# A first attention whose spare steps follow a fixed plan, with the shared expert of two blocks among them

## The chip, the cores and the metric

One core of a Trainium2 chip. The metric is the device time of one execution in microseconds (us). Engine names are those of the profile: PE is TensorE (PEld its weight loads), DVE is VectorE, ACT is ScalarE, POOL is GpSimd, and SP's queue issues most of the DMAs.

## What is computed

Four layers, each an attention or mixer and a feed-forward part, on 8 sequences of 256 tokens of width 256. Each part is added to its input and normalised: `x = layernorm(x + part(x))`. The change lies in the first two parts:

```python
# attention of layer 0: 16 query heads and 4 key heads of width 16, causal
q, k, v = x @ wq, x @ wk, x @ wv          # q and k turned by rope
out = softmax(mask(q @ k.T / 4)) @ v
x = layernorm(x + out @ wo)
# feed-forward part of layer 0
scores = sigmoid(x @ gate_w.T)             # routing to 2 of 4 groups, 8 of 32 experts
routed = (sum over chosen experts of weight * relu2((x @ fc1.T) @ w1.T) @ w2.T) @ fc2.T
shared = relu(x @ shared_up_w.T) ** 2 @ shared_down_w.T
x = layernorm(x + routed + shared)
...
```

## The kernel before

Tokens stay on the chip: `X[b]` holds sequence b as 128 partitions x 2 x 256, and `xT[k]` holds its transpose for a block of two sequences (512 tokens). A transposing step (`transpose_x`, L154) makes `xT` from `X` through a PSUM bank. There are eight PSUM banks, two each under the tags "a", "s", "t" and "o"; a tile of a tag waits until the tile two before it under that tag has been read.

`attn0` (the first attention) is in a region whose order on PE, DVE, ACT and POOL is the order of the Python calls. Its parts are generators, and each `yield` is a step:

- `project(blk)`: for one block, in layer 0 first two transposes, then two products for k (L288, evacuated by DVE at L297), four for q (L288 and L303) and one for v (L308, evacuated by ACT). Nine steps, all in "t" banks.
- `maxima(b)`: three steps, the scores of a sequence (L331) with the mask (L339) in the four "a" and "s" banks, and their row maxima (four `nm` reductions on DVE, L343). POOL then makes `HL` from them.
- `spread(b)`: the maxima are transposed (L355, a "t" bank) and spread out by DVE (`E`, L359).
- `weights(b)`: three steps, the transposed scores (L374) minus the maxima (L382, which needs `E`) in the "a" and "s" banks, and the exponentials `pT` on ACT (L388), with a mask on POOL (L390).
- `finish(b)`: five steps: two for the values (L405, "o" banks), one for the transposes (L416, two "t" banks, read by DVE at L420 and L421 into `att`), one for the transpose of `att` (L431, copied to `aT`), one for the output product (L440), the residual and the norm (L164, L183, L184, POOL's L146 and L147, L190).

The loop over b runs `maxima(b+1)` beside `weights(b)`, and calls `fill` twice in each of the three rounds of a sequence. `fill` takes one step of `finish(b-1)`, then, every second call in most sequences, one of the queue `ahead` (the projection of the block after, and at the end `between`), then one of the queue `sorting`. At sequences 1, 3 and 5 `drain` takes whatever `ahead` still holds, all at once. After the loop, five more `fill` calls finish sequence 7.

`ffn0_shared` is the shared expert of one block: four up steps (L1061, two PE instructions each in turn in an "s" and an "a" bank, relu and square on ACT at L1066 and L1067), then two down steps (L1074, eight PE instructions in an "o" bank, added to `X` at L1079). `ffn0_sort` routes one group of four sequences: products with the gate and fc1 (L977, read by DVE at L981 and ACT into `lat` at L982), a sigmoid (L988), maxima and indices on DVE (L1002 to L1008), ranks by `place` (two small products L879, sums L882 to L888), the experts of the tiles (`r_te`, L928), weights, and then 16 indirect DMAs on POOL (L939) that scatter `lat` to memory. `ffn0_experts` fetches these rows (SP, L1094), and per tile of 128 rows turns them (L1110, copied by ACT at L1112), multiplies by w1 (L1118), squares, multiplies by w2 (L1135) and adds up on DVE (`yg`, L1144 and L1146).

In `attn0` before, the sort of group 0 runs from sequence 5 on in `sorting`, 23 steps in all, with "a" banks for its products; the shared expert of block 0 runs from sequence 7 on in `ahead`. In `ffn0` the shared experts of blocks 1 and 2 run beside the scatter; then come the experts of group 0 (`tiles`), beside the sort of group 1; then block 3, and the experts of group 1 beside the combination of group 0. At the step of block 2 where `next(tiles)` stands, `then()` also queues on SP the weights of the next attention (6 MB and two small vectors, `gq` and `gk`). Their product `gqk` (L1265, DVE) belongs to the next part; the place where it stands in DVE's order is chosen by a scheduler.

Line numbers here and in the prediction are those of this kernel. The profile counts the records of a float32 product twice, so x8 in it is four instructions.

Of the kernel before, what the change touches and what calls it, by code (L numbers as in the profile page):

```python
# [19 lines left out]
NB = 8  # L20
# [3 lines left out]
NBLK = NB * T // BLK  # L24
# [15 lines left out]
class Model:  # L40


    def __init__(self, ctx, tc, ins, out):
# [26 lines left out]
        c = self.const  # L70
        self.X = [c.tile([P, 2, D], F32, name=f"X{b}", tag=f"X{b}") for b in range(NB)]
        self.xT = [c.tile([P, 2, BLK], F32, name=f"xT{k}", tag=f"xT{k}") for k in range(NBLK)]
# [177 lines left out]
    def attn0(self, w, act, start=False, beside=None, between=()):  # L250
# [201 lines left out]
        for rows, tiles in zip(self.lrows, TILES0):  # L452
            for i in range(0, tiles, 3):
                n = min(3, tiles - i)
# [4 lines left out]

        ends, ahead, calls = [], [], [0]

        def step(queue):
            while queue:
                if next(queue[0], queue) is not queue:
                    return
                queue.pop(0)

        def fill(every=2):  # L470
            step(ends)
            calls[0] += 1
            if calls[0] % every == 0:
                step(ahead)
            step(sorting)

        def drain():
            while ahead:
                step(ahead)

        sorting = []
        for _ in project(0):
            pass
        prev = maxima(0)
# [1 line left out]
            next(prev)  # L486
        for b in range(NB):
            nxt = None
            if b == 0 or b % 2 == 1:
                drain()  # L490
                if (b + 3) // 2 < NBLK:
                    ahead.append(project((b + 3) // 2))
            if b + 1 < NB:
                nxt = maxima(b + 1)
            else:
                ahead.append(between)
            if b == NB - 3 and beside:
                sorting.append(beside)
            next(prev, None)
            mine = weights(b)  # L500
            for i in range(3):
                if nxt is not None:
                    next(nxt)
                if b > 1 and i == 0:
                    self.norm_done(b - 2)
                fill(2 if b else 1)
                if i == 0:
                    spread(b)
                next(mine)
                fill(2 if 0 < b < NB - 1 else 1)  # L510
            ends.append(finish(b))
            prev = nxt
        self.norm_done(NB - 2)
# [536 lines left out]
        self.sorted0[g] = slots, expert  # L1050
        yield from self.scatter(self.lrows[g], slots, lambda t, k: lat[:, t, k, :])

    def ffn0_shared(self, w, blk, act, tags=("hs", "relu"), bufs=2):

        nc = self.nc
        xT = self.xT[blk]
        hs = act.tile([P, 4, BLK], F32, tag=tags[0], name="hs", bufs=bufs)
        for m in range(4):
            pu = self.ps("a" if m % 2 else "s")
            for c in range(2):  # L1060
                nc.tensor.matmul(  # L1061
                    pu, w["up"][:, c, m * P : (m + 1) * P], xT[:, c, :],
                    start=(c == 0), stop=(c == 1),
                )
            relu = act.tile([P, BLK], F32, tag=tags[1], name="relu")
            nc.scalar.activation(relu, pu, AF.Relu)  # L1066
            nc.scalar.activation(hs[:, m, :], relu, AF.Square)  # L1067
            yield
        for i in range(2):
            y = self.ps("o").rearrange("p (t d) -> p t d", t=2)  # L1070
            for t in range(2):
                cols = slice((2 * i + t) * P, (2 * i + t + 1) * P)
                for m in range(4):
                    nc.tensor.matmul(  # L1074
                        y[:, t, :], hs[:, m, cols], w["down"][:, m, :],
                        start=(m == 0), stop=(m == 3),
                    )
            X = self.X[2 * blk + i]
            nc.vector.tensor_tensor(X, y, X, ALU.add)  # L1079
            yield  # L1080
# [124 lines left out]
    def ffn0(self, w, act, keep, temp, sort, then, start=False):  # L1205

        w2 = self.load(act, "f0_w2", [P, 32, P], split=4)
        w1, w2 = (x.rearrange("p (g e) f -> p g (e f)", g=4) for x in (w["w1"], w2))
        if start:
            for b in range(NB):
                self.transpose_x(b)
            for _ in self.ffn0_shared(w, 0, act):
                pass
            sort = self.ffn0_sort(w, 0, temp, keep)
        tiles = self.ffn0_experts(w1, w2, 0, act)
        for blk in (1, 2):  # L1220
            for i, _ in enumerate(self.ffn0_shared(w, blk, act)):
                next(sort, None)
                next(sort, None)
                if blk == 1 and i == 1 and not start:
                    self.norm_done(NB - 1)
                if blk == 2 and i == 3:
                    for _ in sort:
                        pass
                    sort = self.ffn0_sort(w, 1, temp, keep)
                if blk == 2 and i == 4:  # L1230
                    next(tiles)
                    then()
        for _ in tiles:
            next(sort, None)
        for _ in sort:
            pass
        put = self.ffn0_combine(w, 0, keep)
        tiles = self.ffn0_experts(w1, w2, 1, act)
        for i, _ in enumerate(self.ffn0_shared(w, 3, act)):
            next(put, None)  # L1240
            if i == 3:
                next(tiles)
        for _ in tiles:
            next(put, None)
        for _ in put:
            pass
        return self.ffn0_combine(w, 1, keep)
# [834 lines left out]
@with_exitstack  # L2082
def tile_layers(ctx: ExitStack, tc: tile.TileContext, ins, out, phases):
    m = Model(ctx, tc, ins, out)
    sides = ("left", "right")
    stack = {}

    keeps, kept = {}, {}

    def open_weights(i):  # L2090
        s = ExitStack()
        load = getattr(m, phases[i] + "_load")
        args = []
        if phases[i] in ("ffn0", "attn3"):
            keeps[i] = ExitStack()
            kept[i] = keeps[i].enter_context(
                tc.tile_pool(name=f"keep{i}", bufs=1, side=sides[i % 2])
            )
            args = [kept[i]]
        if phases[i] == "ffn0":  # L2100
            m.temp = s.enter_context(
                tc.tile_pool(name="temp", bufs=1, side=sides[i % 2])
            )
        pool = s.enter_context(tc.tile_pool(name=f"w{i}", bufs=1, side=sides[i % 2]))
        stack[i] = (s, load(pool, *args))

    open_weights(0)
    m.load_rest()
    left = []
    for i, name in enumerate(phases):  # L2110
        m.last = i == len(phases) - 1
        with tc.tile_pool(name=f"act{i}", bufs=2, side=sides[i % 2]) as act:
            if not m.last and name not in ("ffn0", "attn1"):
                open_weights(i + 1)
            w, start = stack[i][1], i == 0
            engines = COMPUTE | {mybir.EngineType.SP} if name == "ffn0" else COMPUTE
            with tc.manual_schedule(engines=engines) if name in MANUAL else ExitStack():
                if name == "attn0":
                    beside, between = None, iter(())
                    if not m.last:  # L2120
                        wn = stack[i + 1][1]
                        left = beside = m.ffn0_sort(wn, 0, m.temp, kept[i + 1])
                        between = m.ffn0_shared(wn, 0, act, ("qT", "kh0"), bufs=3)
                    m.attn0(w, act, start, beside, between)
                elif name == "ffn0":
                    then = partial(open_weights, i + 1) if not m.last else list
                    left = m.ffn0(w, act, kept[i], m.temp, left, then, start=start)
                elif name == "attn1":

                    def then(i=i):  # L2130
                        keeps[i - 1].close()
                        open_weights(i + 1)

                    m.attn1(w, act, left, then, start=start)
                elif name == "attn3":
                    beside = None
                    if not m.last:
                        beside = partial(m.ffn3_sort, stack[i + 1][1], 0, each=3)
                    left = m.attn3(w, act, kept[i], start=start, beside=beside)
                elif name == "ffn3":  # L2140
                    m.ffn3(w, act, left, start=start)
                    keeps[i - 1].close()
                else:
                    getattr(m, name)(w, act, start=start)
        stack[i][0].close()
# [125 lines left out]
```

## Time and profile before

| | |
|---|---|
| median of 3 runs | 2552.52 us (2549.58 to 2555.33) |
| profiled execution | 2540.15 us, span 2538.4 us |
| PE, PEld | 2225.3 us (88%), 1510.7 us (60%) |
| DVE, ACT, POOL | 1432.9, 1044.6, 916.3 us |
| mean granted clock of PE | 0.945 |
| first attention, ends with the last transpose of X | 281.62 us |
| first scatter of group 0, fetch of its rows | 283.07 us, 304.67 us |
| shared expert of block 3 begins (after the experts of group 0) | 407.10 us |

The span is what the profiler saw of one execution; a busy share is an average over stages that have different limits. In a row of a timeline the columns are the start, the duration, the engine, the line and the operation with what it writes and reads; in brackets stands the idle time before it and what ended it. A row of waits has the waiting instruction, what released it, the sum, the number of times and the longest. The granted clock is the share of full speed at which PE was let run.

### The profile page before, as it was taken

How to read it: one execution, taken by the hardware profiler on the slowest of the kernel's cores; microseconds unless marked ns; L12 is line 12 of the kernel's file. 1: busy time of each engine (PE TensorE's matmuls, PEld its weight loads, DVE VectorE, ACT ScalarE, POOL GpSimd, SP SyncE). 2: the span in 40 equal slices, each digit the busy share in tenths (PEclk: the TensorE clock that was granted, in tenths of full speed). 3: DMA queues.
4: the chain of work that ended last, by engine and by line, in shares of the span. 5: the costliest groups of instructions: out<-in, count | busy, mean ns of one | idle time of the engine just before them, and what ended most of it. 6: DMA issues, size and time to landing. Idle time of an engine off the chain costs nothing. (4 is left out here: it accounts for less than half of the span.)

```text
span 2538.4 us, 36327 instructions
## 1 busy us (share of the span) xinstructions
PE 2225.3 (88%) x12016; PEld 1510.7 (60%) x12016; DVE 1432.9 (56%) x3597; ACT 1044.6 (41%) x3001; POOL 916.3 (36%) x1725
## 2 busy tenths in 40 slices
PE   8998979989999999999999999998887787668990
PEld 4554678856666666666664555555555555457780
DVE  3655276755445444445455444646788878745363
ACT  1223345544445345345342112221576656644450
POOL 1222325344334333333213221000466656833555
PEclk9998999999999999999999999999998978789995
DMA  5000321110000100000070011001000000145673
GB/s 158 1 1 1 118 70 46 34 42 4 3 4 3 52 1 1 1 1 1 15 261 1 0 50 50 2 0 63 40 1 1 1 1 22 42 123 166 210 216 95
DMA packets 92309, 120.76 MB, mean 48 GB/s; under 512 B 9757, under 2 KB 79582, under 8 KB 91102
## 3 DMA queue, kind: packets, MB, share of 16 engines
q1 hardware_dynamic: 82270, 95.75, 11.6%
q0 software_dynamic: 8192, 21.11, 2.8%
q8 instruction: 100, 1.64, 0.3%
q10 hardware_dynamic: 1664, 1.57, 0.2%
q14 instruction: 83, 0.68, 0.1%
HBM read 67.53 MB, written 50.88 MB: 47 GB/s over the span
## 5 line engine op out<-in xcount | busy, mean ns | idle before, releaser
L1372 POOL TENSOR_SCALAR p<-p,rs 128x128 f32<-128x128 f32 (+1 forms) x256 | 104.2, 424 | 293.7 <-DVE rs L1370 289.4
L1362 ACT ACTIVATE p<-ps_s,nm,rq 128x128 f32<-128x128 f32 (+1 forms) x256 | 128.0, 507 | 151.1 <-DVE nm L1360 151.1
L146 POOL TENSOR_SCALAR rsq<-bnmv 128x2 f32<-128x2 f32 x64 | 13.6, 212 | 454.0 <-DVE bnmv L184 446.4
L1290 ACT ACTIVATE sq<-ps_a 128x512 f32<-128x512 f32 x126 | 76.0, 603 | 225.8 <-PE ps_a L1282 225.5
L647 ACT ACTIVATE e<-ps_a,nm 128x128 f32<-128x128 f32 (+1 forms) x256 | 105.9, 435 | 107.7 <-DVE nm L644 93.3
L1291 DVE TENSOR_REDUCE ssk<-sq 128x4 f32<-128x512 f32 x64 | 43.8, 686 | 172.3 <-ACT sq L1290 172.3
L689 POOL TENSOR_SCALAR v<-e,r,nmd 128x128 f32<-128x128 f32 (+1 forms) x256 | 134.7, 537 | 10.0
L1282 PE MATMUL ps_a<-w_a_wq,xT 128*128 128x512 f32 x256 | 121.5, 597 | 11.8 <-DVE k L1304 9.2
L1282 PE MATMUL ps_a<-w_a_wv,xT 128*128 128x512 f32 x256 | 122.2, 600 | 2.1 <-ACT q L1315 2.1
L706 PE MATMUL ps_t<-ident,v 128*128 128x128 f32 x384 | 68.7, 316 | 61.4 <-DVE qT L585 30.1
L1962 PE MATMUL ps_a<-w_f_gup,xTg 128*128 x504 | 112.2, 347 | 10.8 <-DVE xTg L1956 4.2
L681 DVE SCALAR_TENSOR_TENSOR e<-e,c 128x128 f32<-128x128 f32 (+1 forms) x256 | 105.9, 463 | 24.9 <-POOL c L668 24.8
L1291 DVE TENSOR_REDUCE ssq<-sq 128x4 f32<-128x512 f32 x64 | 43.9, 686 | 130.5 <-ACT sq L1290 130.5
L1282 PE MATMUL ps_a<-w_a_wk,xT 128*128 128x512 f32 x248 | 116.5, 593 | 0.0
L1410 PE MATMUL ps_o<-w_a_wo,attT 128*128 128x256 f32 x512 | 111.8, 379 | 0.0
L647 ACT ACTIVATE e<-ps_s,nm 128x128 f32<-128x128 f32 (+1 forms) x256 | 106.8, 451 | 0.0
L1410 PEld LDWEIGHTS ps_o<-w_a_wo,attT 128*128 128x128 f32 x512 | 96.7, 190 | 12.8
L1146 DVE SCALAR_TENSOR_TENSOR yg<-ps_t,xg,yg 128x128 f32<-128x128 f32 x266 | 93.1, 350 | 12.5 <-PE ps_t L1135 3.6
L1349 PE MATMUL ps_s<-kT,qT 128*128 128x256 f32 (+1 forms) x512 | 99.5, 327 | 0.0
L706 PEld LDWEIGHTS ps_t<-ident,v 128*128 128x128 f32 x384 | 49.9, 162 | 81.1 <-issue 31.3
L1396 PE MATMUL ps_o<-pT,V 128*128 128x256 f32 x256 | 79.5, 392 | 19.3 <-ACT pT L120 19.2
L1962 PEld LDWEIGHTS ps_a<-w_f_gup,xTg 128*128 128x128 f32 x504 | 83.0, 198 | 21.3 <-ACT yg L1992 10.7
(403 smaller groups left out, 6116.0 us busy)
## 6 DMA issues: line engine op xcount, KB each, us to landing
rows<-zero SPq DMA_DIRECT2D x42, 384.0 KB, 4.4
xg<-rows SPq DMA_DIRECT2D x42, 384.0 KB, 3.4
outs<-yg SPq DMA_DIRECT2D x42, 384.0 KB, 3.6
w_f_gup<-in_f_gup SPq DMA_DIRECT2D x8, 768.0 KB, 9.7
w_f_w<-in_f_w SPq DMA_DIRECT2D x8, 512.0 KB, 5.4
w_f_down<-in_f_down SPq DMA_DIRECT2D x8, 384.0 KB, 9.0
w_f_up<-in_f_up SPq DMA_DIRECT2D x5, 512.0 KB
lrows<-zero SPq DMA_DIRECT2D x12, 204.0 KB, 5.7
```

The source lines that it names most:

```text
L647: nc.scalar.activation(e[:, s, j * nk : (j + 1) * nk], sc[s][:, j, :], AF.Exp, bias=nm[:, s, j : j + 1], scale=1.0, accum_out=sums[:, s, j ...
L681: nc.vector.scalar_tensor_tensor(d[:, s, h, :], u.e[:, s, h, 1, :], u.c[:, s, h : h + 1], d[:, s, h, :], ALU.mult, ALU.add,)
L689: nc.gpsimd.tensor_scalar(u.v[:, s, h, :], d[:, s, h, :], u.r[:, s, h, 0:1], nm[:, s, h : h + 1], ALU.mult, ALU.add,)
L706: nc.tensor.transpose(ps[:, s, c, :], x, self.ident)
L1146: nc.vector.scalar_tensor_tensor(acc[j], y, c, acc[j], ALU.mult, ALU.add)
L1282: nc.tensor.matmul(ps, self.xt(u.b, t, c), w[which][:, c, u.cols], start=(c == 0), stop=(c == 1),)
L1291: nc.vector.tensor_reduce(out, sq, AX.X, ALU.add)
L1349: nc.tensor.matmul(sc[:, j, :], u.qT[:, h0 + j, qc * P : (qc + 1) * P], u.kT[:, h0 + j, 0:nk], start=(j == 0), stop=False,)
L1362: nc.scalar.activation(u.p[qc][:, h0 + j, :], sc[:, j, :], AF.Exp, bias=nm[:, j : j + 1], scale=r[:, j : j + 1], accum_out=u.sums[qc][:, h ...
L1372: nc.gpsimd.tensor_scalar(u.p[qc][:, j, :], u.p[qc][:, j, :], ri[:, j : j + 1], 1.0, ALU.mult, ALU.mult,)
L1410: nc.tensor.matmul(y[:, t, :], attTs[b][:, h, t * P : (t + 1) * P], w["wo"][:, h, :], start=(h == 0), stop=(h == 15),)
L1962: nc.tensor.matmul(ps, xT[j][:, c, :], w["gup"][:, bass.ds(er[j], 1), c, :].rearrange("p o f -> p (o f)"), start=(c == 0), stop=(c == 1),)
```

## The change

The plan: in place of every second call, `fill(n)` takes n steps of `ahead`, and a list of six numbers per sequence says how many. Sequence 0 takes all nine steps of the projection of block 1; a pair of an odd and an even sequence takes 5 and 4; `drain` goes. In the last three sequences (5, 6, 7) `ahead` holds the shared experts of blocks 0 and 1, four steps per sequence, and the five calls after the loop take the rest. `ffn0_shared` yields once more in the middle of each down step, so that a block is eight steps. It and the sort of group 0 now use "t" banks for their products in `attn0`, and "a" and "s" are left to the scores. In `ffn0` only block 2 stands beside the scatter; the rest of the sort of group 0 is taken at its fifth step, and the experts' first turn comes after its seventh.

```diff
-        ends, ahead, calls = [], [], [0]
+        ends, ahead, sorting = [], [], []
...
-        def fill(every=2):
+        def fill(n):
             step(ends)
-            calls[0] += 1
-            if calls[0] % every == 0:
+            for _ in range(n):
                 step(ahead)
             step(sorting)
 
-        def drain():
-            while ahead:
-                step(ahead)
-
-        sorting = []
...
         for b in range(NB):
             nxt = None
-            if b == 0 or b % 2 == 1:
-                drain()
-                if (b + 3) // 2 < NBLK:
-                    ahead.append(project((b + 3) // 2))
+            if (b == 0 or b % 2 == 1) and (b + 3) // 2 < NBLK:
+                ahead.append(project((b + 3) // 2))
             if b + 1 < NB:
                 nxt = maxima(b + 1)
+            if b == 0:
+                steps = (3, 1, 1, 1, 1, 2)
+            elif b % 2 == 1 and b < NB - 3:
+                steps = (1, 1, 1, 1, 0, 1)
             else:
-                ahead.append(between)
-            if b == NB - 3 and beside:
-                sorting.append(beside)
+                steps = (1, 0, 1, 1, 0, 1)
+            if b == NB - 3:
+                ahead.extend(between)
+                if beside:
+                    sorting.append(beside)
             next(prev, None)
             mine = weights(b)
             for i in range(3):
...
-                fill(2 if b else 1)
+                fill(steps[2 * i])
                 if i == 0:
                     spread(b)
                 next(mine)
-                fill(2 if 0 < b < NB - 1 else 1)
+                fill(steps[2 * i + 1])
...
-    def ffn0_shared(self, w, blk, act, tags=("hs", "relu"), bufs=2):
+    def ffn0_shared(self, w, blk, act, tags=("hs", "relu"), bufs=2, banks="as"):
...
-            pu = self.ps("a" if m % 2 else "s")
+            pu = self.ps(banks[m % len(banks)])
...
+                if t == 0:
+                    yield
             X = self.X[2 * blk + i]
             nc.vector.tensor_tensor(X, y, X, ALU.add)
             yield
...
-            for _ in self.ffn0_shared(w, 0, act):
-                pass
+            for blk in range(2):
+                for _ in self.ffn0_shared(w, blk, act):
+                    pass
             sort = self.ffn0_sort(w, 0, temp, keep)
         tiles = self.ffn0_experts(w1, w2, 0, act)
-        for blk in (1, 2):
-            for i, _ in enumerate(self.ffn0_shared(w, blk, act)):
-                next(sort, None)
-                next(sort, None)
-                if blk == 1 and i == 1 and not start:
-                    self.norm_done(NB - 1)
-                if blk == 2 and i == 3:
-                    for _ in sort:
-                        pass
-                    sort = self.ffn0_sort(w, 1, temp, keep)
-                if blk == 2 and i == 4:
-                    next(tiles)
-                    then()
+        for i, _ in enumerate(self.ffn0_shared(w, 2, act)):
+            next(sort, None)
+            next(sort, None)
+            if i == 1 and not start:
+                self.norm_done(NB - 1)
+            if i == 4:
+                for _ in sort:
+                    pass
+                sort = self.ffn0_sort(w, 1, temp, keep)
+            if i == 6:
+                next(tiles)
+                then()
...
         for i, _ in enumerate(self.ffn0_shared(w, 3, act)):
             next(put, None)
-            if i == 3:
+            if i == 5:
                 next(tiles)
...
-                        left = beside = m.ffn0_sort(wn, 0, m.temp, kept[i + 1])
-                        between = m.ffn0_shared(wn, 0, act, ("qT", "kh0"), bufs=3)
+                        left = beside = m.ffn0_sort(wn, 0, m.temp, kept[i + 1], "t")
+                        between = [
+                            m.ffn0_shared(wn, blk, act, ("qT", "kh0"), bufs=3, banks="t")
+                            for blk in range(2)
+                        ]
```

More of the change, by code (lines that the diff above doesn't have):

```diff
@@ L2118, in tile_layers @@
                 if name == "attn0":
-                    beside, between = None, iter(())
+                    beside, between = None, []
                     if not m.last:
                         wn = stack[i + 1][1]
-                        left = beside = m.ffn0_sort(wn, 0, m.temp, kept[i + 1])
-                        between = m.ffn0_shared(wn, 0, act, ("qT", "kh0"), bufs=3)
+                        left = beside = m.ffn0_sort(wn, 0, m.temp, kept[i + 1], "t")
[3 more added lines that the diff above has]
+                        ]
                     m.attn0(w, act, start, beside, between)
```

## The prediction

> **What bounds the kernel now.** I read the page first, then a table of windows over the first 380 us, then the waits and timelines of single engines where that table showed holes. From the page, the busy tenths and the granted clock of TensorE, 40 slices of 63.5 us:
>
> ```profile
> PE   8998979989999999999999999998887787668990
> ...
> PEclk9998999999999999999999999999998978789995
> ```
>
> PE sets the pace nearly everywhere, so a shift of one stage is carried to the end. The change touches only slices 0 to 8. There the windows (columns: PE, PEld, DVE, ACT, POOL busy, then clock, DMA share, GB/s) say where PE has room:
>
> ```profile
> 160.00:180.00 20.00, 19.99 (x141) 11.75 (x142) 12.68 (x22) 3.82 (x7) 3.78 (x8) 1.00 0.00 1
> 180.00:200.00 20.00, 18.23 (x112) 11.76 (x108) 7.66 (x16) 7.73 (x13) 2.42 (x4) 0.83 0.00 1
> 200.00:220.00 20.00, 16.70 (x131) 8.24 (x130) 12.53 (x53) 6.48 (x11) 6.57 (x14) 0.91 0.00 1
> 220.00:240.00 20.00, 16.37 (x94) 6.91 (x90) 14.66 (x64) 6.78 (x13) 5.89 (x12) 0.84 0.01 2
> 240.00:260.00 20.00, 16.27 (x65) 7.50 (x61) 6.83 (x27) 7.77 (x14) 3.60 (x7) 0.84 0.00 1
> ...
> 320.00:340.00 20.00, 13.56 (x95) 12.96 (x94) 12.77 (x71) 7.67 (x14) 3.51 (x5) 0.86 0.25 89
> ```
>
> From 60 us to the end of sequence 4 (175 us) PE runs at full clock with under 1 us idle per 20. From sequence 5 on it is idle about 2 to 4 us per 20 and its clock falls. One-microsecond windows show seven idle stretches of 1.7 us or more between 180 and 345 us; each is followed within 3 us by about 3.4 us at half clock (once 6). Stretches of 0.6 and 1.28 us are not; one of 1.23 was, for 7 us.
>
> What follows the attention is a chain. These are the first and last scatter on POOL and the fetch on SP's queue:
>
> ```profile
> 283.07 1.24 POOL L939 DMA_INDIRECT lrows<-lat,r_slots  x1 [2.06 <-DVE lat L1046]
> ...
> 302.31 0.96 POOL L939 DMA_INDIRECT lrows<-lat,r_slots  x1 [0.30 <-issue]
> ```
> ```profile
> 304.67 1.40 SPq L1094 DMA_DIRECT2D xg<-lrows  x3
> 306.12 0.94 SPq L132 DMA_DIRECT2D w_a_wq<-in_a_wq  x2
> ```
>
> The last transpose of sequence 7 (281.62) is followed 1.45 us later by 16 scatters (20.2 us), the fetch comes at 304.67, and about 2.2 us later the experts can start. They are then held by one DVE instruction, from the waits of DVE between 300 and 345 us:
>
> ```profile
> DVE gqk L1265 <- DMA w_a_gk<-in_a_gk: 8.5, 1, 8.5
> ```
>
> It waits until 326.07 for a load queued behind 6 MB of weights, and every yg (L1144, L1146) is behind it.
>
> **What the Trainium skill says.** "TensorE: Matmul & The Clock Gate", part 1 on the HAM clock gate: the clock has two rates, and an idle window of about 3.4 us halves it until a busy one has passed. The trace agrees on the length (206.6 to 209.7), but 1.76 us idle (to 236.74) sufficed here; I use the trace. The same page, "Step-by-step: what each phase is for": matmuls stay in program order, only weight loads are pulled ahead. The trace agrees: L374 waited 2.84 us to 253.15 for a bank and nothing behind it ran. "ScalarE: Activation LUTs", "What ACT_TABLE_LOAD costs": 1283 ns to switch tables; the trace has 1.28 us at 194.58 and 201.67.
>
> **The change, part by part.** Prices at full clock, from the PE timeline: one projection or up step (L288, L1061) 1.9 us; a half down step of 8 records 1.8; L405 1.0 and 1.85; L416 1.0; L431 0.5; L440 1.8; L374 with L382 1.85 if nothing is late; L331 with L339 2.07 or 1.6; a transpose L154 0.55.
>
> *A. The fixed plan, sequences 0 to 4.* The work is the same; the drains at sequences 1, 3, 5 (7.6 us of PE in a lump) are spread out. But in sequences 1 to 4 one step now stands between L416 and L374, and both it and L416 use the two "t" banks. The first L416 bank is free only when DVE has done L420 and L421, which queue behind four L343:
>
> ```profile
> 76.70 1.04 PE L416 MATMUL ps_t<-ident,oS 128*128 128x128 f32 x8
> 77.67 0.69 PE L374 MATMUL ps_a<-qT,kT 32*128 32x512 f32 x1
> ```
> ```profile
> 78.38 0.68 DVE L343 TENSOR_REDUCE nm<-ps_s 128x2 f32<-128x512 f32 x1
> 78.98 0.25 DVE L420 RECIPROCAL ri<-ps_t 128x16 f32<-128x16 f32 x1
> 79.26 0.42 DVE L421 TENSOR_TENSOR att<-ps_t,ri 128x256 f32<-128x256 f32 x1
> ```
>
> PE is ready at 77.7, the bank at 79.7: a new wait of 2.05 us, and all PE work is behind it. L374 had been slowed there by the same L343 (77.67 to 80.38, 2.7 for 1.85); that 0.85 goes. Net 1.2 x 4 = +4.8. In sequences 1 and 3 the third L331 came at 81.41 but was held by pT until about 82.4 (L331 and L339 took 2.5 for 1.6); a step now covers that: -1.8. In 2 and 4 the second L331 loses its cover: +0.7. Sequence 0: -0.5. Then the clock: 2.05 us is over the 1.76 that halved it, and half clock for 3.4 us costs 1.7, of which I take 0.5 as hidden by the waits for E (0.6 in each sequence) that fall inside: 1.2 x 4 = +4.8. Bounds 0 (the gap split over two windows) and 13.6 (two windows each, as at 192.6 to 199.8). A = +8.0.
>
> *B. Sequence 5, from one L339 to the next (174.53 to 207.79, 33.3 us).* Its parts add up to 22.6 at full clock, so 10.7 is waiting and half clock. Now it gets four up steps (+7.6). The sort's banks go from "a" to "t", so the waits of L331 and L374 for lat (0.55 and 1.23) go. New is the 2.05 behind L416; of the 2.0 us that L331 waited for pT behind the table switch, 1.4 stays after an up step; one half-clock window 1.7. Sum 22.6 + 7.6 + 2.05 + 1.4 + 1.7 = 35.3: +2.1.
>
> *C. Sequence 6 to the last norm (207.79 to 281.6, 73.8 us).* Without shared steps the parts are 39.2, with 3.7 for the last norm. Before, 18.6 of shared work lay inside (block 0 and half of block 1's ups), so 16.0 was lost. Now 23.0 lies inside: eight half downs 14.4, four ups 7.6, an early piece of block 2. Waits left: 3.2 at L154 of sequence 5, since its "t" bank must first be read by the rank sums L884, which stand behind the norm and a new L1079 (0.69) on DVE; some 2.1 in small ones (pT, att, the norm of 6). The wait for r_te (2.84) goes with the own bank, those for E (1.28, 1.76) are covered by steps ahead of the spread. ACT has 1.23 per up step more, but ends each within the next L374. 39.2 + 23.0 + 5.3 + 1.7 (one window) = 69.2: -4.6.
>
> The attention so ends 8.0 + 2.1 - 4.6 = 5.5 us later, with block 1 done in it.
>
> *D. The scatter.* Both orders hand out 23 steps of the sort before ffn0, so the scatters start as far behind the last norm as before, and POOL's and SP's queues have the same order. The fetch shifts by 5.5. Of block 1's 11 us that left, nothing is gained: PE has only 14.5 us of work (block 2, the second sort's products) under the 25 us of chain, where before it was full. Splitting the down step costs nothing for the same reason; if that cover were gone it would be one L1079, 0.7.
>
> *E. The experts' start.* In the built order gqk now stands behind 19 yg instead of ahead of all, and the second sort's ACT work (lat, table switch), for which L1118 waited 2.16 at 317.07, is done during the scatter. Counted from the fetch (0): first turn 2.7, at half clock after the idle stretch; half a down 6.3, ups to 10.0, first L1135 10.2. DVE then needs 1.5 per L1135, 3.0 for the indices and 1.9 for the ranks, and the seventh L1135 comes at 26.5; gqk's load has landed by then (21.4). Before, the seventh came at 342.04, 37.4 after the fetch, with the sort equally far. -10.9 (bounds -4, if DVE is late with the sort, and -13). Later tiles, and group 1, whose scatter ended (398.45) before the fetch at 409.71, keep their times; the half down in front of its first tile hides under PE-bound work.
>
> Sum: +5.5 - 10.9 = -5.4 us. Against the profiled execution, 2540.15 us for a span of 2538.4, that is 2534.8; the median of the runs is 2552.52, 12.4 us (0.5%) above it, and the same difference gives 2547.1 there. About 0.2% (5.1 us) is what a measurement can tell from no change; the forecast lies just over it.
>
> **The rivals.** *Clock stays up*: the 2 us gaps of A, B and C do not halve it. For it: PE is full around them. Against: seven of seven stretches over 1.7 us. A +3.2, B +0.4, C -6.3, E -10.9: -13.6, 2538.9.
> *The experts do not give it back*: with gqk gone DVE is still bound by the second sort beside yg (DVE 16.32 of 20 between 340 and 360). E only -5: +0.5, 2553.0.
> *Slower: the bank wait behind L416 halves the clock for two windows each time.* Place: sequences 1 to 5. For it: 192.6 to 199.8 and 254.5 to 260.5 were such cases, in this very stage. Against: the six others were one window. A 3.2 + 13.6, B +3.8, C -2.9, E -10.9: +6.8, 2559.3. It decides once the attention ends over 16.0 us later (10.9 + 5.1).
> That the change does not do what it says is excluded for the order: the built instructions show the steps and banks in their places.
>
> **How the numbers follow.** Forecast 0.45, spread from -11 to -1, just over half of it beyond -5.1: 0.25 faster, 0.20 same. Clock stays up 0.22, faster. Experts give little 0.17: 0.13 same, 0.04 slower. Slower 0.16. So faster 0.47, same 0.33, slower 0.20. The range runs from just below the clock rival to the slower one, 2537 to 2560; the forecast's own range is 2541 to 2551.
>
> **What would show it.** A: waits of L288 for L421 of about 2 us, four times, and clock under 1.00 between 70 and 170. B, C: no wait for lat or r_te, the last transpose of X near 287. D: first scatter 1.4 us behind it. E: gqk's wait gone or under 2 us, the seventh L1135 some 27 us after the fetch. I am wrong if L288 does not wait behind L416, or if the attention ends earlier than 281.6.

## The result, and the profile after

The changed kernel takes 2539.83 us (median of 6 runs, 2533.1 to 2544.39), the kernel before 2552.26 beside it (6 runs, 2549.58 to 2555.76): ratio 0.9948, 95% interval 0.9932 to 0.9964, so some 13 us faster. The forecast was 2547.1, range 2537 to 2560.

The profiled execution of after took 2538.78 us, span 2537.1: only 1.3 us less than that of before. The tenths of TensorE and its clock, from the page:

```profile
PE   8998789989999999999999999998888777678990
...
PEclk9999999999999999999999999999988988789995
```

The third and fourth digits of PEclk (about 127 to 254 us) have gone from 98 to 99. In the windows (columns as before: PE, PEld, DVE, ACT, POOL busy, clock, DMA share, GB/s) the filling shows from 200 to 260 us, and the hole has moved under and behind the scatter:

```profile
180.00:200.00 20.00, 17.61 (x127) 10.35 (x126) 8.16 (x17) 8.10 (x14) 2.83 (x6) 1.00 0.00 1
200.00:220.00 20.00, 19.06 (x111) 10.11 (x114) 11.40 (x44) 9.82 (x16) 3.78 (x8) 0.83 0.00 1
220.00:240.00 20.00, 18.95 (x140) 11.64 (x136) 14.92 (x58) 6.68 (x13) 5.05 (x11) 1.00 0.00 1
240.00:260.00 20.00, 17.29 (x91) 7.49 (x95) 9.27 (x37) 8.87 (x16) 3.98 (x8) 0.91 0.01 1
...
300.00:320.00 20.00, 11.13 (x70) 10.14 (x71) 5.21 (x41) 8.78 (x16) 8.40 (x11) 0.74 0.67 247
320.00:340.00 20.00, 14.95 (x118) 14.43 (x118) 16.46 (x80) 8.81 (x17) 3.29 (x4) 0.91 0.37 132
```

The first and last scatter on POOL, and the fetch on SP's queue, are 2.0 us later than before:

```profile
285.05 1.24 POOL L937 DMA_INDIRECT lrows<-lat,r_slots  x1 [2.05 <-DVE lat L1044]
...
304.32 0.96 POOL L937 DMA_INDIRECT lrows<-lat,r_slots  x1 [0.31 <-issue]
```
```profile
306.69 1.40 SPq L1094 DMA_DIRECT2D xg<-lrows  x3
```

Behind L416 PE now waits, as priced, for the bank that DVE reads after four L343 (PE, then DVE, sequence 1):

```profile
77.94 1.04 PE L416 MATMUL ps_t<-ident,oS 128*128 128x128 f32 x8
81.07 2.80 PE L288 MATMUL ps_t<-xT,w_a_wk 128*128 128x512 f32 x4 [2.09 <-DVE att L421]
```
```profile
79.62 0.68 DVE L343 TENSOR_REDUCE nm<-ps_s 128x2 f32<-128x512 f32 x1
80.21 0.25 DVE L420 RECIPROCAL ri<-ps_t 128x16 f32<-128x16 f32 x1
80.50 0.42 DVE L421 TENSOR_TENSOR att<-ps_t,ri 128x256 f32<-128x256 f32 x1
```

The wait of gqk is gone from DVE's waits between 300 and 345 us. What stands there is a product of the second sort. PE could not give it yet, since its bank was held by ACT's copy of the products before (L980), which has to wait for the scatters (shown at the last experiment):

```profile
DVE r_lg L979 <- PE ps_a L975: 11.1, 1, 11.1
DVE yg L1144 <- PE ps_t L1135: 3.9, 2, 2.2
DVE r_lg L988 <- ACT r_sc L986: 2.4, 1, 2.4
```

The forecast so looks nearly confirmed: the attention ends 2 us later, gqk is gone, the experts begin sooner. The experiments show that gqk is not the source of the gain.

### The profile page after: what moved, and what is told of

The parts are those of the page before. It is cut to its first block, busy times and chain, and to the rows that moved or that the text cites. A ratio compares the mean times of both kernels' runs of the same rounds, so it can differ in the third digit from the quotient of the medians.

```text
span 2537.1 us, 36262 instructions
## 1 busy us (share of the span) xinstructions
PE 2204.6 (87%) x11960; PEld 1498.3 (59%) x12016; DVE 1434.5 (57%) x3597; ACT 1045.4 (41%) x3001; POOL 919.3 (36%) x1725
## 5 line engine op out<-in xcount | busy, mean ns | idle before, releaser
L146 POOL TENSOR_SCALAR rsq<-bnmv 128x2 f32<-128x2 f32 x64 | 13.7, 213 | 459.4 <-DVE bnmv L184 451.9
L1282 PE MATMUL ps_a<-w_a_wq,xT 128*128 128x512 f32 x256 | 122.7, 602 | 12.4 <-DVE k L1304 9.4
L1282 PE MATMUL ps_a<-w_a_wv,xT 128*128 128x512 f32 x256 | 120.5, 593 | 1.0 <-ACT q L1315 1.0
L1282 PE MATMUL ps_a<-w_a_wk,xT 128*128 128x512 f32 x248 | 116.5, 593 | 0.0
L1962 PEld LDWEIGHTS ps_a<-w_f_gup,xTg 128*128 128x128 f32 x504 | 83.9, 200 | 29.1 <-ACT yg L1992 10.3
L1146 DVE SCALAR_TENSOR_TENSOR yg<-ps_t,xg,yg 128x128 f32<-128x128 f32 x266 | 93.1, 350 | 13.7 <-PE ps_t L1135 3.3
```

Source lines behind the costliest of these rows:

```text
L1146: nc.vector.scalar_tensor_tensor(acc[j], y, c, acc[j], ALU.mult, ALU.add)
L1282: nc.tensor.matmul(ps, self.xt(u.b, t, c), w[which][:, c, u.cols], start=(c == 0), stop=(c == 1),)
L1962: nc.tensor.matmul(ps, xT[j][:, c, :], w["gup"][:, bass.ds(er[j], 1), c, :].rearrange("p o f -> p (o f)"), start=(c == 0), stop=(c == 1),)
```

## The experiments

All marks come from PE's timeline and SP's fetch. As executions start up to 2.9 us apart, two columns count from the first L405. "Attention": to the last transpose of X. "First" and "seventh": L1135 after the fetch. "attn1": to the first product of the next attention (L1282). Each median is of 5 to 22 runs, and each ratio is to the kernel before, run beside it. After and e2 have the same instructions up to the fetch, and yet their attentions differ by 4.7 us: half clock covers 17.1 us of it in after and 6.8 in e2. So a difference of less than some 5 us between the attentions of two traces shows little by itself.

| kernel | median | ratio, 95% interval | attention | first | seventh | attn1 |
|---|---|---|---|---|---|---|
| before, first profile | 2552.26 | 1 | 212.9 | 13.8 | 37.4 | 438.8 |
| e12 before, second profile | (2554.32, one run) | - | 212.8 | 22.0 | 40.3 | 441.6 |
| after | 2539.83 | 0.9948 (0.9932-0.9964) | 213.7 | 10.3 | 28.9 | 431.4 |
| e1 before, gk early | 2550.96 | 0.9998 (0.9988-1.0008) | 215.2 | 21.3 | 39.9 | 443.9 |
| e5 before, gqk late | 2551.27 | 1.0002 (0.9995-1.0008) | 212.6 | 21.2 | 39.7 | 440.8 |
| e9 before, ups first | 2552.66 | 1.0003 (0.9995-1.0011) | 213.0 | 19.0 | 37.3 | 438.8 |
| e10 e9 + gqk late | 2552.39 | 0.9993 (0.9982-1.0004) | 211.8 | 21.9 | 40.3 | 440.8 |
| e2 after, gqk back | 2546.38 | 0.9978 (0.9969-0.9987) | 209.0 | 10.3 | 37.0 | 436.5 |
| e3 after, block 0 only, gk early | 2538.03 | 0.9951 (0.9932-0.997) | 204.2 | 21.5 | 40.5 | 433.4 |
| e6 after, block 0 only | 2539.94 | 0.9963 (0.995-0.9977) | 205.1 | 22.2 | 40.9 | 434.9 |
| e8 after, shared banks | 2539.62 | 0.9961 (0.9947-0.9974) | 217.4 | 10.3 | 28.6 | 436.5 |
| e11 after, old plan | 2542.77 | 0.9962 (0.9948-0.9975) | 213.6 | 10.3 | 28.6 | 432.8 |
| e4 after, no step behind L416 | 2526.8 | 0.991 (0.9894-0.9926) | 205.5 | 10.3 | 30.1 | 424.1 |
| e7 e6 + e4 | 2532.79 | 0.9935 (0.9921-0.9948) | 196.9 | 19.6 | 38.2 | 424.1 |

**e1: is gqk's wait the gain?**

```diff
         w2 = self.load(act, "f0_w2", [P, 32, P], split=4)
+        self.g1 = {x: self.load(self.small, f"a1_{x}", [P, 1]) for x in ("gq", "gk")}
...
-        w["gq"] = self.load(pool, "a1_gq", [P, 1])
-        w["gk"] = self.load(pool, "a1_gk", [P, 1])
+        w.update(self.g1)
```

> The kernel before, with one edit: gq and gk, 512 bytes each, are loaded into the small pool right behind w2, ahead of the fetch and of the 6 MB of weights, so that gqk (L1265) has nothing to wait for. Nothing else moves. Theory (most of the gain of the change is this one wait of 8.5 us on DVE, which the new order avoids): the seventh L1135 comes 29 us after the fetch instead of 37.4, and the time is 6 to 9 us under the kernel before, ratio 0.9965 to 0.9976. Rival (the gain is block 1's work, put into holes of the attention): within 2 us of the kernel before.

The time did not move. gqk now waited 2.7 us at 289.2, harmlessly, and yet the first L1135 came 21.3 us after the fetch instead of 13.8. The reason shows on ACT, in the relus of block 2 (in brackets: idle before, and who ended it):

```profile
300.70 0.60 ACT L1066 ACTIVATE relu<-ps_s 128x512 f32<-128x512 f32 x1 [9.41 <-PE ps_a L1061]
...
305.65 0.60 ACT L1066 ACTIVATE relu<-ps_a 128x512 f32<-128x512 f32 x1 [3.69 <-remote]
...
308.51 0.60 ACT L1066 ACTIVATE relu<-ps_s 128x512 f32<-128x512 f32 x1 [1.60 <-remote]
```

PE's up steps for these were finished at 298.9, 300.7 and 302.4 (starts 297.06, 298.78, 300.50, 1.88 each). In the built program L1066 waits for PE alone. "remote" means that the profile names no releaser. But the trace keeps the times at which PE's semaphore, the counter that this wait reads, counts up, and it does so at 300.68, 305.63 and 308.49, 20 ns ahead of each relu. So ACT did not stand still with all its work ready: PE's signals came 1.7 to 6.1 us after the ends of PE's steps. PE's half downs wait for these relus, and the second sort's products and the first tile stand behind them.

**e2: gqk's wait put back into after.**

```diff
                 if half == 0 and i == 0:
+                    if g == 0 and j == 0:
+                        self.gqk = self.small.tile([P, 1], F32, tag="gqk", name="gqk", bufs=1)
+                        nc.vector.tensor_tensor(self.gqk, *self.gs, ALU.mult)
                     nc.vector.tensor_scalar(acc[j], y, c, None, ALU.mult)
```

> The changed kernel, with gqk written by hand just ahead of the first yg (L1144), where it stood in the kernel before; its loads stay behind the 6 MB. Theory: a wait of 7 to 9 us of DVE for gk comes back, and the time is 6 to 9 us above the changed kernel, so 4 to 7 us under the kernel before (ratio 0.997 to 0.9985). Rival (the gain is in the attention): as the changed kernel, ratio 0.995.

Some 7.7 us of the gain are lost (0.9978 against 0.9948), the theory's figure. DVE's waits:

```profile
DVE gqk L1146 <- DMA w_a_gk<-in_a_gk: 11.7, 1, 11.7
```

So this wait costs time in the changed kernel and none in the kernel before. The next experiments say why.

**e3: block 1 back beside the scatter, gk early.**

```diff
-                            for blk in range(2)
+                            for blk in range(1)
...
-        for i, _ in enumerate(self.ffn0_shared(w, 2, act)):
+        for blk in (1, 2):
+            for i, _ in enumerate(self.ffn0_shared(w, blk, act)):
```

> The changed kernel with block 0 alone as filling: block 1 goes back beside the scatter, as before, while plan and own banks stay; gq and gk are loaded early as in the first experiment, since the built order would otherwise put gqk back ahead of the first yg. The prediction held that block 1 in the attention gains nothing, as PE is empty under the scatter: theory 1 then has the attention end some 8 us earlier than in the changed kernel (less work in it), PE fuller under the scatter, and the time up to 8 us under the changed kernel (ratio 0.9915 to 0.994). Rival (the holes of sequences 5 to 7 are waits of PE, which block 1 fills for nothing): the attention ends at the same time within 3 us, and so does the whole, ratio 0.994 to 0.996; slower still if block 1 delays the second sort.

Neither came as written: the attention is 9.5 us shorter, as the theory said, but the time stays at the changed kernel's. ACT idles as in e1 (relus at 287.55, 292.50, 295.36, with PE done at 285.9, 287.6, 289.4), and what the attention gained is lost between the fetch and the first L1135 (21.5 against 10.3).

**e4: no step between L416 and L374.**

```diff
-                steps = (1, 1, 1, 1, 0, 1)
+                steps = (1, 1, 0, 2, 0, 1)
             else:
-                steps = (1, 0, 1, 1, 0, 1)
+                steps = (1, 1, 0, 1, 0, 1)
```

> The changed kernel with the plan of sequences 1 to 7 altered so that no step stands between L416 and L374: (1,1,0,2,0,1) and (1,1,0,1,0,1), as many steps as before in each. Theory (the five waits of 2.09 us of L288 and L1059 behind L416 are pure loss, and each fourth or so halves the clock): they go, L374 is late by 0.85 instead, and the attention ends 5 to 8 us earlier; time 5 to 8 us under the changed kernel, ratio 0.992 to 0.993. Rival (L374 needs the same DVE work, four L343, so the wait only moves to it, and the pT wait comes back where the step was): within 2 us of the changed kernel.

Some 10 us under the changed kernel by the ratios, whose intervals do not overlap; in the trace the attention is 8.2 us shorter (3.5 against that of e2, which has as little half clock, 6.8 us) and attn1 begins 7.3 us earlier, the theory's size. PE goes on where it had waited 2.09 us, while DVE works through the same queue (L421 at 79.35):

```profile
76.80 1.04 PE L416 MATMUL ps_t<-ident,oS 128*128 128x128 f32 x8
77.77 0.69 PE L374 MATMUL ps_a<-qT,kT 32*128 32x512 f32 x1
```

The rival, that L374 takes the wait over, is out: L374 and L382 take 2.7 us here (77.77 to 80.48, where L431 follows) for 1.85, as in the kernel before, not 2.09 more. One such wait is left, of a product of the sort in sequence 5. The 2 us of the ratio beyond 7.3 lie later and are not explained.

**e5: gqk behind the 19th yg in the kernel before.**

```diff
                 else:
+                    if (g, j, half, i) == (0, 2, 0, 3):
+                        self.gqk = self.small.tile([P, 1], F32, tag="gqk", name="gqk", bufs=1)
+                        nc.vector.tensor_tensor(self.gqk, *self.gs, ALU.mult)
                     nc.vector.scalar_tensor_tensor(acc[j], y, c, acc[j], ALU.mult, ALU.add)
```

> The kernel before, with gqk written by hand between the 19th and the 20th yg, where the changed kernel has it; no load is moved. In the first experiment the early load of gq and gk had a side effect (ACT stood idle three times, 1.8, 3.7 and 1.6 us, with nothing to wait for in the program), so it did not settle the question. Theory: gqk's wait of 8.5 us was on the path of the kernel before; the seventh L1135 comes 29 to 32 us after the fetch, and the time is 4 to 8 us under the kernel before, ratio 0.997 to 0.9985. Rival (the wait covered others, such as the products and ACT work of the second sort, so nothing is gained): within 2 us of the kernel before.

The rival holds, to a tenth of a per cent. ACT is idle for 4.9 and 2.3 us here too, the first L1135 comes at 326.2. In the first profile of before gqk was free at 326.07: with ACT's idle time in front of it, the first yg comes no earlier than gk lands. The two waits lie side by side, and removing one leaves the other.

**e6: block 0 only, gqk late.**

```diff
-                            for blk in range(2)
+                            for blk in range(1)
...
+                    if (g, j, half, i) == (0, 2, 0, 3):
```

> The changed kernel with block 0 alone as filling (block 1 beside the scatter, as before), gqk written by hand behind the 19th yg, no load moved. Theory: the attention ends 12 us earlier than in the changed kernel, as in the third experiment, PE is full under the scatter, and without ACT's three idle stretches the first L1135 comes some 14 us after the fetch: 5 to 8 us under the changed kernel, ratio 0.992 to 0.993. Rival (block 1 is neutral wherever it stands, since PE's sum of work sets the end): as the changed kernel, ratio 0.994 to 0.996.

The rival is nearest: 0.9963, just outside its range and not separable from after. The attention is 8.5 us shorter, the first L1135 11.9 us later after the fetch; ACT's relus stand still with no small load involved, so e1's load was not their cause. And 9.4 us of the gain stay, by the ratio, though block 1 is not in the attention.

**e7: e6 with e4's plan.**

```diff
-                            for blk in range(2)
+                            for blk in range(1)
...
-                steps = (1, 1, 1, 1, 0, 1)
+                steps = (1, 1, 0, 2, 0, 1)
```

> The sixth experiment with the plan of the fourth (no step between L416 and L374). Theory: the gains add up, the attention ends 8 us or more earlier than in the sixth, and the time is 2516 to 2522, ratio 0.986 to 0.9885. Rival (they overlap in the same stretch): not under the fourth, ratio 0.990 to 0.992.

Up to attn1 it equals e4 (424.1 both); the theory of added gains is out. In the whole it is some 6 us slower than e4 by the ratios, whose intervals just overlap. The two traces go together to 1450 us, are 1.5 us apart from 1470 on and some 3 to 7 after 2070, where both issue the same instructions; that is not explained.

**e8: the banks of before for the filling.**

```diff
-                        left = beside = m.ffn0_sort(wn, 0, m.temp, kept[i + 1], "t")
+                        left = beside = m.ffn0_sort(wn, 0, m.temp, kept[i + 1])
...
-                            m.ffn0_shared(wn, blk, act, ("qT", "kh0"), bufs=3, banks="t")
+                            m.ffn0_shared(wn, blk, act, ("qT", "kh0"), bufs=3)
```

> The changed kernel with the banks of the kernel before for the filling: shared expert in the attention on a and s, sort on a, everything else as changed. The prediction priced the own banks at the waits of L331 and L374 for lat (0.55 and 1.23 us) and of L374 for r_te (2.84), less 2.05 behind L416 in sequences 5 to 7. Theory: these come back, 3 to 6 us above the changed kernel, ratio 0.996 to 0.9975. Rival (a filling step on a or s makes the next L331 or L374 wait for ACT's two passes over its bank, so the banks are the larger part of the gain): 8 us or more above the changed kernel, ratio 0.998 or more. Second rival (the t banks are as crowded): within 2 us of the changed kernel.

The first theory fits: 3.3 us by the ratios, though the intervals overlap, and 3.8 in the attention by the traces, which is within what two executions differ by. L374 again waits 2.8 us for r_te.

**e9: the eight up steps of blocks 1 and 2 first, then the downs, in the kernel before.**

```diff
+        both = [self.ffn0_shared(w, blk, act) for blk in (1, 2)]
+        for n, which in enumerate([0] * 4 + [1] * 4 + [0] * 2 + [1] * 2):
+            next(both[which])
```

> The kernel before with one order changed on PE and ACT: beside the scatter, the four up steps of block 2 come right behind those of block 1, and all eight half downs after them; the sort, the fetch and gqk keep their places. The traces of the first, third, fifth and sixth experiment show ACT idle for 5 to 8 us in front of relus of block 2 that start 13 us or more after the first scatter, until 3.5 us after the last; the profile of the kernel before is the one that shows none. Theory (the usual execution of the kernel before has these idle stretches, and the changed kernel gains by having block 2's ups done 3 us after the first scatter): the ups are done 14 us after the first scatter at the latest, no idle stretch of ACT over 1 us holds them, the first L1135 comes some 14 us after the fetch instead of 21, and the time is 5 to 10 us under the kernel before, ratio 0.996 to 0.998. Rival (ACT's idle stretches are made up for later): within 2 us of the kernel before.

Nothing gained. ACT now runs through (last relu of the eight at 295.30), but the hold has moved to DVE:

```profile
304.96 0.69 DVE L1079 TENSOR_TENSOR X<-ps_o,X 128x512 f32<-128x512 f32 x1 [19.95 <-remote]
307.23 0.69 DVE L1079 TENSOR_TENSOR X<-ps_o,X 128x512 f32<-128x512 f32 x1 [1.58 <-remote]
```

PE began the 32 records of down steps at 295.10, so the first y of 16 was ready before 299. PE stood 3.62 us and went on at 305.79 (in e10 the same wait, 5.58 us, is put down to L1079, which frees the o bank). So it is not ACT, nor the relu: what waits for PE late in the scatter is held up. PE's down steps end at 298.72 and 302.17, its semaphore counts up at 304.93 and 307.20, and DVE starts 30 ns later each time.

**e10: e9 and gqk late.**

```diff
+        for n, which in enumerate([0] * 4 + [1] * 4 + [0] * 2 + [1] * 2):
...
+                    if (g, j, half, i) == (0, 2, 0, 3):
```

> The ninth experiment with gqk behind the 19th yg, as in the fifth. Theory: with ACT's idle stretches gone the first yg comes before gk has landed, so that gqk's wait counts here, though it did not in the fifth: a further 4 to 8 us, ratio 0.993 to 0.9955, about the changed kernel's. Rival (gqk's wait counts nowhere): as the ninth, within 2 us.

The rival, within the intervals: DVE was held before L1079 until 304.83 (its y was ready before 297), and gqk's place has no effect while it is.

**e11: the plan of before in sequences 0 to 4.**

```diff
-            if (b == 0 or b % 2 == 1) and (b + 3) // 2 < NBLK:
...
+            if b == 0 or b % 2 == 1:
+                while ahead:
+                    step(ahead)
...
-                steps = (3, 1, 1, 1, 1, 2)
...
+                steps = (1, 1, 1, 1, 1, 1)
...
+                steps = (0, 1, 0, 1, 0, 1)
```

The `while` is the drain. It stands at sequence 7 too, where in the kernel before the queue is empty; here it takes the whole shared expert of block 1 at once.

> The changed kernel with the plan and the drains of the kernel before in sequences 0 to 4 (one step each second call); filling, banks and sequences 5 to 7 as changed. The prediction priced the new plan at +8.0 us there, the two profiles show +4.3 (first unit of sequence 5 at 180.0 for 174.5, of which 1.2 is a later start). Theory: the attention ends 4 to 8 us earlier and the time is 4 to 8 us under the changed kernel, ratio 0.9915 to 0.993. Rival (the plan's cost is taken back in sequence 5, which begins with less left over): within 2 us of the changed kernel, ratio 0.994 to 0.996.

The number is the rival's, attention 213.6 against 213.7, but the edit does not test it. Sequence 5's first unit comes 4.3 us earlier from the first L405 (105.8, as in before, against 110.1), and the output product of sequence 5 (L440) 7.4 us earlier (155.8 against 163.2). The lead is lost in sequence 7, where PE does block 1 in one lump:

```profile
233.24 10.04 PE L1062 MATMUL ps_t<-xT,w_f_up 128*128 128x512 f32 x16 [3.02 <-DVE r_upto L885]
243.11 7.39 PE L1075 MATMUL ps_o<-w_f_down,hs 128*128 128x256 f32 x32
```

So what the plan of sequences 0 to 4 costs at the end of the attention stays open.

**e12: a second profile of the kernel before, no edit.**

> The kernel before once more, for a second profile. Theory (its first profile was an unusual execution, 12 us quicker than its median, since ACT had no idle stretch under the scatter): this one shows ACT idle for 5 us or more in front of block 2's relus, the first L1135 some 21 us after the fetch, gqk's wait under 2 us, and a span of some 2550. Rival (the 12 us lie in the last third, after 1755 us): first L1135 at fetch + 14 and a gqk wait of 8.5 us, as in the first profile.

As the theory said: first L1135 at fetch + 22.0, gqk executes at 325.1 with no wait listed, span 2552.6. First the relus of block 2 on ACT in this execution, then in the first profile of the same program:

```profile
299.22 0.60 ACT L1066 ACTIVATE relu<-ps_s 128x512 f32<-128x512 f32 x1 [11.20 <-issue]
299.85 0.63 ACT L1067 ACTIVATE hs<-relu 128x512 f32<-128x512 f32 x1
305.58 0.60 ACT L1066 ACTIVATE relu<-ps_a 128x512 f32<-128x512 f32 x1 [5.10 <-remote]
```
```profile
296.21 0.60 ACT L1066 ACTIVATE relu<-ps_s 128x512 f32<-128x512 f32 x1 [7.68 <-PE ps_s L1061]
296.84 0.63 ACT L1067 ACTIVATE hs<-relu 128x512 f32<-128x512 f32 x1
297.93 0.60 ACT L1066 ACTIVATE relu<-ps_a 128x512 f32<-128x512 f32 x1 [0.46 <-PE ps_a L1061]
```

And what PE made of it, second profile of before, then after:

```profile
306.89 5.81 PE L1074 MATMUL ps_o<-w_f_down,hs 128*128 128x256 f32 x14 [5.63 <-ACT hs L1067]
312.54 3.42 PE L977 MATMUL ps_a<-w_f_gate_fc,xT 128*128 128x160 f32 x24
...
326.35 1.91 PE L1135 MATMUL ps_t<-w_f_w,hg 128*128 x8
```
```profile
294.57 1.89 PE L1072 MATMUL ps_o<-w_f_down,hs 128*128 128x256 f32 x8
307.56 2.50 PE L975 MATMUL ps_a<-w_f_gate_fc,xT 128*128 128x160 f32 x8 [11.10 <-issue]
309.85 0.42 PE L1110 MATMUL ps_a<-ident,xg 128*128 128x128 f32 x1
...
316.96 1.13 PE L1135 MATMUL ps_t<-w_f_w,hg 128*128 x8
```

In before, 14 records of block 2's downs, then 24 of the sort and more, still lie ahead of the first tile when PE's late signals have come. In after, all but 8 records of the downs and 8 of the sort are behind PE by 296.5, and PE idles until the scatter is over, so late signals in that time cost it nothing. What it idles for is ACT's copy of the second sort's products:

```profile
306.71 1.50 ACT L980 COPY lat<-ps_a 128x768 f32<-128x768 f32 x2 [17.71 <-DMA lrows<-lat,r_slots]
```

`lat` has one buffer, and the scatters of the first group still read it; both "a" banks are held until this copy. A second buffer for `lat` might lift this limit; it was not tried.

The part of the theory that explained the 12 us between before's first profile and its median was wrong: up to attn1 the two profiles differ by 2.8 us. The rest lies in the last stage: from the last w_f_gate product to the last transpose of xg the first profile took 178.5 us, e12 190.5, after 192.7.

## Why the prediction was right or wrong

The sign and the range were right; the forecast was 8 us short of the ratio's 13.3. That this is the figure of the rival "clock stays up" is luck: half of the halvings came, and the reason given for the largest term was false. The terms one by one, after against e12, from the first L405:

*A, +8.0 predicted, +4.3 measured* (to sequence 5's first unit, 110.1 for 105.8). The wait was right: 2.05 priced, 2.09 found, in each of the four sequences. Two terms were mis-sized. For the clock the prediction had "1.2 x 4 = +4.8"; two halvings came (at 82.0 and 136.6). e2, e3 and e8 have the same PE instructions up to here and had one; they come to this place at 108.4, while after and e6, with two, come at 110.1 and 110.0. So a halving costs 1.7 here, and without any +0.9 is left, where the prediction had +3.2. e4 shows where the loss lies: without the step behind L416 this stretch is 102.6, 3.2 us under before.

*B and C, -2.5 predicted, -3.4 measured.* B came to +2.9 (36.2 for 33.3; predicted +2.1), C to -6.3 (67.4 for 73.7; -4.6). The own banks are worth 3.8 of it by e8, if the clock did not make that difference.

*Attention, +5.5 predicted, +0.9 measured*. With its later start it ends 2.0 us behind that of before's first profile. In e2, with the same instructions and less half clock, it takes 3.8 us less than in e12 and ends at 276.5, which is under the 281.6 that the prediction named as a sign of being wrong.

*D.* The scatter followed the last transpose of X by 1.46 us, as before.

*E, -10.9 predicted, -11.4 measured* (seventh L1135 28.9 us after the fetch for 40.3; predicted 26.5). The size is luck, since the figure for before came from an unusual execution (37.4) and the one for after was missed by 2.4; the reason was false, and this is the step that failed: the prediction said that the experts "are then held by one DVE instruction", gqk. e1, e5 and e10 remove its wait and gain nothing. It also said that of block 1's 11 us "nothing is gained". In all profiles of before and its variants but the first, PE's signals to ACT or DVE come late near the end of the scatter, and the shared work that depends on them, which PE has in order ahead of the first tile, is held. Moving block 1 into the attention took that work out of the way: it costs 8.5 us in the attention and saves 11.9 behind the fetch (after against e6), so the net is small. gqk's wait would have come out then, as e2 shows (7.7 us); the built order of after, with gqk behind 19 yg, prevents that. So the late gqk is needed but is not the source of the gain. The second sort's ACT work was not "done during the scatter" either: the copy into `lat` ran at 306.71 and the table switch at 310.96, both behind the fetch, and the first L1135 came at 10.3 for the 10.2 predicted all the same.

*Sum.* Predicted -5.4; measured to the seventh L1135 -10.4 (265.7 for 276.1), to attn1 -10.2. Of the 5.0 us between, in this pair of traces, the attention holds 4.6 (A 3.7, B and C 0.9), E the rest. About 3 us of the ratio's 13.3 arise later; executions differ there by more than that, so these were not assigned.

*By parts*, by the ratios: block 1 back costs 3.8 us (e6) and shared banks 3.3 (e8), each with an interval that overlaps that of after. Most of the 13.3 is therefore there without block 1 in the attention: up to attn1, e6 is 6.7 us ahead of e12, all of it in the attention, though PE does the same shared work there in both (24 and 32 records of ups and downs). The plan, the banks and the new places of the filling make it together. How much of it is the plan is not shown, since e11 (3.6) changed sequence 7 as well.

The rival "experts do not give it back" is out (E -11.4), and so is "slower": no wait behind L416 cost two clock windows. The price of a halving was wrong in its chance. "Seven of seven stretches over 1.7 us" in one trace became 10 of 27 waits of 2.09 us over eight kernels.

## What to carry to other kernels

Before a wait is given the credit for a later start, take a second profile: one execution can lack the delay that the others have, and then a wait that normally lies beside it looks like the bound. Where an engine seems to stand still with its input ready, read when the semaphore that it waits for counted up. Work that PE has in order ahead of a late chain is safer done before that chain starts, even if it costs nearly as much there as it saves (8.5 and 11.9 us here), because late signals are then off the path. A filling step is best put where its bank is free already; moving it by one position (e4) is worth 10 us here, and at 0.991 it is the fastest kernel of this study.

## What the runs showed of the hardware

*PE's signals come late near the end of the scatter.* While POOL issues its 16 indirect DMAs, relus of ACT (e1, e3, e5, e6, e7, e12) or L1079 of DVE (e9, e10) start up to 8 us after PE's records of what they wait for have ended (e10: 296.63, started at 304.83). In all eight, the last held instruction starts 3.4 to 3.7 us after the last scatter's issue (e12: 305.58 after 301.96; e9: 307.23 after 303.50). The semaphore times of the traces say where the delay lies. In e12 three up steps of block 2 end on PE at 297.39, 299.11 and 300.82, and PE's semaphore counts up at 305.56, 305.62 and 305.68; in the first profile of before the same counts come 0.01 to 0.02 us after the ends. Where the count is on record, the held engine starts 20 to 30 ns behind it. The profile's ends of PE instructions are modelled, but steps that start 1.72 us apart would hardly end within 0.12 us; so the records speak for a late signal, and against late work of ACT, DVE or PE.

Of nine profiles with such work in that time, the first of before alone shows no late signal. The changed kernel has them too, and so have e2, e4, e8 and e11, at no cost (after: PE's step ended at 294.73, counted at 298.72, L979 at 298.75). The first profile of before is also the only one in which hardly any counts are missing (PE 2571 of 2573; in e12 2505 of 2517, and of ACT's 1828 only 1723), so it is not shown that the taking of the profile has no part in the delay.

The Trainium skill, "SBUF — State Buffer", "Who interferes with whom", lists no port that PE or ACT shares with another engine, so this doesn't look like a port. "Runtime: NRT & Kernel Launch", "Instruction fetch mechanics", says that each sequencer fetches its instructions by DMA, mostly hidden. The trace does not show a late fetch either: the instruction queues that it records moved nothing between 293 and 307 us of e12. The cause stays open; a kernel whose scatter goes another way was not tried.

*The clock.* Apart from the last 60 us of each execution, half clock came in stretches of 3.4, 6.8, 10.2 or 13.7 us and once 17.1, all multiples of 3.41. The same 2.09 us wait of sequence 1 was followed by one in after, e2 and e6 and not in e3 and e8. "TensorE: Matmul & The Clock Gate", part 1 on the HAM clock gate, says that the window is free-running, 3413 ns long, not tied to the kernel's start: the lengths agree, and so does the change from run to run. It also asks for an idle window of about 3.4 us before the clock halves; here 2.09 us of idle time sufficed, in 10 of 27 cases.
